# Two levels of the seven-product scheme for the queries of a self-attention stage, and GpSimd in written order

## The chip, the cores and the metric

The kernel runs on one core of one Trainium2 chip. The metric is the device time of one execution in microseconds (us), as the median of several executions. A core has TensorE (PE in the profile, with its weight loads as PEld), VectorE (DVE), ScalarE (ACT), GpSimd (POOL) and SyncE (SP, which here only issues DMAs). Each takes its instructions in order; they wait for one another through semaphores.

## The reference, cut to what matters

One decoder layer in float32: self-attention, cross-attention and a feed-forward part, each followed by a layer norm. The change touches the self-attention, and in it the queries.

```python
# x: 32 x 64 x 512 (2048 tokens); 32 query heads, 8 key/value heads, head size 128
q = (x @ wq.T).reshape(b, l, 32, 128)            # the queries
q, k = apply_rope(q), apply_rope(k)
k_full = concat([k_cache[block_idx], k[0]])      # 512 cached + 64 new keys = 576
v_full = concat([v_cache[block_idx], v[0]])
scores = einsum('bhld,bhtd->bhlt', q, k_full) / sqrt(128)
out = einsum('bhlt,bhtd->bhld', softmax(scores), v_full)
x = layernorm(x + out @ wo.T)
x = layernorm(x + cross_attention(x, ctx_4096))  # not touched
x = layernorm(x + feed_forward(x))               # not touched
```

## The kernel before, in words

**Stages.** Self-attention is the first stage, some 1,800 us of the execution; then come the cross-attention's keys and values, its units, and the feed-forward part. The self-attention's work is cut into 128 *units* n: 8 key groups g, in each 4 token blocks tb of 512 tokens, in each 4 heads h (`REP`). A *block* b is the 4 units of one (g, tb), so there are 32 blocks of four units. Feature-major query tiles `qT` of a block hold 4 heads x 512 tokens.

**A unit.** For each of 4 tiles i of 128 queries: TensorE makes the scores `s` (two matmuls of 288 columns, L834; two PSUM buffers of two banks each), VectorE takes the negated maximum `nmax` (L839), ScalarE the exponential with the sum `den` (L842), VectorE the reciprocal (L851), the scaling of `p` (L857) and a transpose in 32x32 blocks into `T` (L865, `turn`). A tile's transpose is issued after the next tile's maximum. At the unit's end 16 DMAs on SP's queue (`move`, L877) bring `T` to `pT`, and two units later TensorE multiplies it with the values (`po`, L885) in two parts, two or three chunks of 512 columns each. After an odd unit `shared_values` adds the keys that two heads share, and ScalarE copies two heads to `oT` (L908).

**Queries and output projection.** Both are products of 512-wide matrices, in one level of the seven-product scheme (Strassen's in Winograd's form): 7 products of quarters in place of 8. One product is four matmuls of 128x128 weights and 256 moving columns (`Product.mul`, L354). Operand sums are made by GpSimd (`token_sums` for the tokens, `load_left` for the query weights, `output_sums` for the attention's output, `load_right` for wo). The queries of block b + 1 are computed during block b (`q_step`), the projection of an earlier block too (`w_step`). Each of the two has one PSUM bank: tags `q` and `w`. The results are added up by ScalarE copies and VectorE adds, which `flush` issues right after the product (`steps`: at most one product in each of four places of a unit: after the scores of tiles 0, 1, 2 and 3; the values come in before the places 1 and 3).

**Order.** In this stage the order of TensorE, VectorE and ScalarE is the written one (`manual_schedule`); GpSimd's and SP's instructions are put in an order by a planner at build time. In the cross-attention GpSimd's order is the written one as well, and its queries are already made in two levels (`DeepQueries`, L493 to L535): 49 products of 128x128 weights and 128 moving columns, in two sets: 7 steps of four matmuls and 7 steps of three.

Gathers of the next group's cached keys and values are issued on GpSimd's queue in units 4, 5, 6 and 8 of a group; `rotate` (VectorE and GpSimd) turns the keys in unit 9.

Of the kernel before, what the change touches and what calls it, by code (L numbers as in the profile page):

```python
# [9 lines left out]
F32 = mybir.dt.float32  # L10
I32 = mybir.dt.int32
AF = mybir.ActivationFunctionType
ALU = mybir.AluOpType
# [3 lines left out]
P = 128  # L17
DIM = 512
NH, NKV, HD = 32, 8, 128
REP = NH // NKV  # L20
NT = 2048
# [31 lines left out]
def decoder_layer(  # L53
    ctx: ExitStack,
    tc: tile.TileContext,
    x: bass.AP,
    xT_in: bass.AP,
    encT_in: bass.AP,
    cos: bass.AP,
    sin: bass.AP,  # L60
# [63 lines left out]
    def rows(src, tb):  # L124
        return src[tb * TB : (tb + 1) * TB, :].rearrange("(p j) f -> p j f", p=P)
# [150 lines left out]
    def load_right(src, name, eng, queue=nc.sync, first=None, held=None):  # L276

        w = first or load_right_first(src, name, queue)
        for i in range(3, 8):
            w[i] = big.tile([P, 2, HF], F32, tag=f"wo{i}", name=f"{name}_{i}")  # L280
        b12 = w[5]
        for dst, (k, n) in ((w[3], (1, 1)), (b12, (0, 1))):
            load_quarter(dst, src, k, n, queue)
        sums = lambda: right_sums(
            eng, w[1], b12, w[2], w[3], {1: w[5], 2: w[6], 3: w[7], 4: w[4]}
        )
        if held is None:
            sums()
        else:
            held.append(sums)  # L290
        return w
# [390 lines left out]
    with ExitStack() as ph:  # L682
# [2 lines left out]
        psum.append(ph.enter_context(tc.tile_pool(name="sps", bufs=1, space=PSUM)))  # L685
        sc = ph.enter_context(tc.tile_pool(name="sc", bufs=2, space=PSUM))
        sb = ph.enter_context(tc.tile_pool(name="sa", bufs=2))

# [39 lines left out]
        def load_group(g, queue=nc.scalar):  # L730
            ws = []
            for tag, src in (("wk", wkT), ("wv", wvT)):
                w = kv.tile([P, NC, HD], F32, tag=tag, name=f"{tag}{g}", bufs=1)
                queue.dma_start(
                    out=w, in_=src[:, g * HD : (g + 1) * HD].rearrange("(c p) n -> p c n", p=P)
                )
                ws.append(w)
            wkv_cur[g] = ws
# [22 lines left out]
        def gather_values(g, t):  # L761
            gather(g, vs[g], v_rows, t)
# [61 lines left out]
        units = [(g, tb, h) for g in range(NKV) for tb in range(NTB) for h in range(REP)]  # L824
        qTs, Ts, pTs, oTs, pos, ps_ = {}, {}, {}, {}, {}, {}

        def scores(n, i):


            g, tb, h = units[n]  # L830
            u = f"{g}_{tb}_{h}_{i}"
            s = sc.tile([P, 2, 512], F32, tag="sc", name=f"s{u}")
            for a in range(2):
                nc.tensor.matmul(  # L834
                    s[:, a, :HALF], qTs[n // REP][:, units[n][2], i * P : (i + 1) * P],
                    kTs[g][:, a * HALF : (a + 1) * HALF], start=True, stop=True,
                )
            nmax = small.tile([P, 1], F32, tag="nmax", name=f"nmax{u}")
            nc.vector.tensor_reduce(nmax, s[:, :, :HALF], AX.XY, ALU.max, negate=True)  # L839
            p = sb.tile([P, NKEY], F32, tag="p", name=f"p{u}", bufs=4)  # L840
            den = small.tile([P, 1], F32, tag="den", name=f"den{u}")
            nc.scalar.activation(  # L842
                p.rearrange("q (a k) -> q a k", a=2), s[:, :, :HALF], AF.Exp,
                bias=nmax, accum_out=den,
            )
            if i == 0:
                Ts[n] = sb.tile([P, NBK, TPB, SQ], F32, tag="T", name=f"T{g}_{tb}_{h}")
                flush()
            else:
                turn(n, i - 1)  # L850
            nc.vector.reciprocal(den, den)  # L851
            if n < REP or n >= N - REP and i % 2:


                nc.scalar.activation(p, p, AF.Copy, scale=den)  # L855
            else:
                nc.vector.tensor_scalar(p, p, den, None, ALU.mult)  # L857
            ps_[n, i] = p
            if i == TPB - 1:
                turn(n, i)  # L860

        def turn(n, i):


            nc.vector.transpose(  # L865
                Ts[n][:, :, i, :], ps_.pop((n, i)).rearrange("q (b k) -> q b k", k=SQ)
            )
# [56 lines left out]
        def columns(g):  # L924
            return slice(g * REP * HD, (g + 1) * REP * HD)
# [40 lines left out]
        def flush():  # L966
            while reads:
                reads.pop(0)()

        load_group(0, nc.sync)  # L970
        cs2 = kc.tile([P, 1], F32, name="cs2")
        sn2 = kc.tile([P, 1], F32, name="sn2")
# [51 lines left out]
        nc.vector.tensor_tensor(t[4], q[1, 0], t[2], sub)  # L1024
        nc.vector.tensor_tensor(c[0, 1], z, c[0, 1], ALU.add)
        tok[1] = token_operands(xTs[1])
        wo_cur[0] = load_right(woT[columns(0), :], "wo0", nc.gpsimd, first=wo_cur[0])

        def last_products(i):
            if i == 7:  # L1030
# [6 lines left out]
        begin.close()  # L1037

        ph.enter_context(tc.manual_schedule(engines={
            mybir.EngineType.PE, mybir.EngineType.DVE, mybir.EngineType.Activation  # L1040
        }))

        short = {0, 1, 2, *range(N - REP, N - 1)}


        gathers = {4: 0, 5: 1, 6: 2, 8: 3}  # L1050
        for n in range(N):
            b, h = divmod(n, REP)
            g, r = units[n][0], n % PER
            if r == REP and g + 1 < NKV:
                load_group(g + 1)
            if r in gathers and g + 1 < NKV:
                gather_keys(g + 1, gathers[r])
            if 0 < n <= PER:


                b2, j = divmod(n - 1, TPB)
                nc.scalar.dma_start(out=acc[b2][:, j, :], in_=rows(x, b2)[:, j, :])
            if r == 2 * REP and g + 1 < NKV:
                later.append(lambda g=g: new_keys(g + 1))
            if r == 2 * REP + 1 and g + 1 < NKV:
                rotate(g + 1)
                later.append(lambda g=g: cached_keys(g + 1))


            b2, k = b + 2, h - (b == 0)  # L1070
            if b2 < NB and k in (0, 1):
                if k == 0:
                    xTs[b2] = token_room(b2, f"xT{b2}")
                load_pieces(xTs[b2], xT_in, b2 % NTB, 2 * k, 2 * k + 1)
            if n >= N - REP:

                if n == N - REP:
                    encT[0] = big.tile([P, NC, TB], F32, tag="qT", name="encT0", bufs=2)
                    kvw[0], kv_loads, kv_sums = kv_left_parts(0, "wq")
                load_pieces(encT[0], encT_in, 0, h)  # L1080
                for load in kv_loads[3 * h : 3 * h + 3]:
                    load()
                if n == N - 2:
                    kv_sums()
            steps = {0: "qwqw", 1: "qw q", 2: "wqwq", 3: "w qw"}[h]

            def step(place):
                if n < REP:

                    i = {(0, 0): 7, (0, 2): 4}.get((n, place))  # L1090
                    if i:
                        last_products(i)
                        if i == 4:
                            token_sums(xTs[1], "tx1", nc.gpsimd)
                    elif (n, place) in ((0, 1), (0, 3), (1, 0), (1, 1), (1, 2), (2, 0), (2, 2)):
                        q_step(n)
                elif steps[place] == "q":
                    q_step(n)
                elif steps[place] == "w":
                    w_step(b - 2 if h < 2 else b - 1)  # L1100
                flush()

            def spare_bank():

                if n % 2 == 0 and later:
                    later.pop(0)()

            scores(n, 0)
            step(0)
            spare_bank()  # L1110
            scores(n, 1)
            if n - 1 in short:
                move(n - 1, (3,), nc.gpsimd)
            if n >= 2:
                values(n - 2, 0, 2 if n % 2 == 0 else 3)
            step(1)
            scores(n, 2)
            step(2)
            if r in gathers and g + 1 < NKV:
                gather_values(g + 1, gathers[r])  # L1120
            scores(n, 3)
            if n >= 2:
                values(n - 2, 2 if n % 2 == 0 else 3, NKT)
                if n % 2:
                    shared_values(n - 2)
            step(3)
            spare_bank()
            if h == REP - 1:
                if b + 2 < NB:
                    g2, tb2, _ = units[(b + 2) * REP]  # L1130
                    if tb2 == 0:
                        wq_cur[g2] = load_left(wqT[:, columns(g2)], f"wq{g2}", nc.gpsimd)
                    tok[b + 2] = token_sums(xTs.pop(b + 2), f"tx{g2}_{tb2}", nc.gpsimd)
                elif b + 2 > NB:
                    encR[0] = token_sums(encT[0], "te0", nc.gpsimd)
            move(n, (0, 1, 2) if n in short else range(NQD))
# [47 lines left out]
    with ExitStack() as ph:  # L1184
# [6 lines left out]
        bz = cb.tile([P, DIM], F32, name="bz")  # L1191
        pe = cb.tile([P, 1], F32, name="pe")
        wo_cur = {}
        flat = "p a b c -> p (a b c)"
        wl = (
            wqs.rearrange(flat).rearrange("p (j i n) -> p j i n", j=4, i=7),
            cb.tile([P, 3, 7, P], F32, name="wlb"),
# [665 lines left out]
```

## Time and profile before

| | |
|---|---|
| time of 3 runs, median (lowest to highest) | 3007.59 us (3006.82 to 3008.73) |
| the profiled execution's own time | 3004.51 us |
| its span, first to last instruction | 3002.7 us |
| mean granted clock of TensorE | 0.999 of full speed |
| TensorE busy | 2977.4 us, 99% of the span |
| VectorE busy | 2127.5 us, 71% |
| ScalarE busy | 1128.1 us, 38% |
| GpSimd busy | 1218.9 us, 41% |
| DMA, mean over the span | 139 GB/s |

The span is what the trace can be asked about. Busy is the time in which an engine had an instruction under way, without what only issues DMAs or waits on semaphores. In the profile a float32 matmul is two instructions (a product of four matmuls is "x8"). Matmuls overlap in the pipeline, so the cost of one is read from the distance between starts, not from its duration. A line such as `L857 DVE TENSOR_SCALAR p<-p,den` is the operation of line 857 on VectorE which writes tile `p`. "idle before" is time in which the engine waited ahead of the instruction, with what ended the wait.

### The profile page before, as it was taken

The page shows a single profiled execution, that of the slowest core. Times are in us where ns is not written, and L with a number is a line of the kernel's source. Part 1 is how long each engine was busy: PE and PEld are TensorE (multiplying, and loading weights), DVE is VectorE, ACT ScalarE, POOL GpSimd, SP SyncE. Part 2 cuts the span into 40 slices and gives each one's busy share as a digit, 9 for nine tenths or more (in the row PEclk, how much of TensorE's full clock was granted, in tenths as well). Part 3 has the DMA queues.
Part 4 walks back from the last instruction along what each step waited for, and adds up shares of the span by engine and source line. Part 5 has one row for each costly group of instructions (what it writes and reads, how often), then busy time and mean ns, then how long its engine had stood idle before and what let it go on. Part 6 is the DMA issues. An engine that isn't in the chain of part 4 may idle for free.

```text
span 3002.7 us, 46451 instructions
## 1 busy us (share of the span) xinstructions
PE 2977.4 (99%) x16144; PEld 2330.4 (78%) x16144; DVE 2127.5 (71%) x3907; ACT 1128.1 (38%) x2767; POOL 1218.9 (41%) x1024
## 2 busy tenths in 40 slices
PE   8999999999999999999999999999999999999998
PEld 6777777777777777777777768999999999999964
DVE  6787777777787777787787774636656666666686
ACT  4322223223223323323223232334455555555564
POOL 5222322321321321321321223667577577567532
PEclk9999999999999999999999999999999999999999
DMA  6554444444444444444444454666555455445420
GB/s 186 128 131 126 114 115 121 115 115 120 115 115 120 116 114 121 116 114 120 116 115 113 97 124 136 243 247 204 177 179 179 160 183 192 163 160 184 136 81 36
DMA packets 224042, 416.59 MB, mean 139 GB/s; under 512 B 48001, under 2 KB 103425, under 8 KB 215617
## 3 DMA queue, kind: packets, MB, share of 16 engines
q1 hardware_dynamic: 208720, 385.69, 45.0%
q0 software_dynamic: 4304, 19.01, 1.8%
q10 hardware_dynamic: 10784, 8.92, 1.0%
q8 instruction: 130, 2.13, 0.3%
q14 instruction: 104, 0.84, 0.1%
HBM read 206.60 MB, written 33.82 MB: 80 GB/s over the span
## 4 chain that ended last, share of the span: by engine, by line
PE 91%; DVE 3%; POOL 2%; SPq 2%; ACT 1%; DMA 1%; issue 0%; DVEq 0%; ACTq 0%; POOLq 0%
PE po L885 17%; PE s L834 16%; PE sx L1412 2%; PE pox L1495 2%; PE qx_1x L493 2%; PE qx_0x L493 2%; PE qx_2x L493 2%; PE qx_3x L493 2%; PE w_1y L354 1%; PE q_3y L354 1%; PE w_0y L354 1%; PE q_2y L354 1%; PE w_3y L354 1%; PE q_0y L354 1%; PE q_1y L354 1%; SPq L160 1%
## 5 line engine op out<-in xcount | busy, mean ns | idle before, releaser
L842 ACT ACTIVATE p<-s,nmax 128x576 f32<-128x576 f32 x512 | 379.1, 740 | 1210.7 <-DVE nmax L839 1155.4
L834 PE MATMUL s<-kT,qT 128*128 128x288 f32 x2048 | 574.7, 406 | 0.5 <-ACT p L842 0.5
L885 PE MATMUL po<-pT,v 128*128 128x512 f32 (+1 forms) x1280 | 549.0, 602 | 2.4 <-DMA acc<-in_x 1.9
L834 PEld LDWEIGHTS s<-kT,qT 128*128 128x128 f32 x2048 | 387.7, 190 | 100.6 <-issue 17.5
L839 DVE TENSOR_REDUCE nmax<-s 128x1 f32<-128x576 f32 x512 | 384.0, 750 | 58.6 <-PE s L834 57.2
L865 DVE STREAM_TRANSPOSE T<-p 128x576 f32<-128x576 f32 x512 | 394.4, 770 | 12.2 <-ACT p L855 7.4
L885 PEld LDWEIGHTS po<-pT,v 128*128 128x128 f32 (+1 forms) x1280 | 213.4, 189 | 202.0 <-issue 174.8
L857 DVE TENSOR_SCALAR p<-p,den 128x576 f32<-128x576 f32 x488 | 302.0, 619 | 17.1
L325 POOL TENSOR_TENSOR so<-oT,oT 128x512 f32<-128x512 f32 x32 | 40.7, 1272 | 545.3 <-ACT oT L908 545.2
L851 DVE RECIPROCAL den<-den 128x1 f32<-128x1 f32 x512 | 83.9, 164 | 224.8 <-ACT p L842 216.1
L328 POOL TENSOR_TENSOR so<-oT 128x512 f32<-128x512 f32 x32 | 40.7, 1271 | 310.3 <-PE w_1y L354 92.8
L249 POOL TENSOR_TENSOR tx<-xT 128x512 f32<-128x512 f32 x31 | 40.7, 1314 | 199.0 <-PE q_3z L354 63.3
L1444 ACT ACTIVATE exps<-exps,denx 128x64 f32<-128x64 f32 x480 | 121.0, 338 | 0.0
L1515 ACT ACTIVATE oTx<-pox,bv 128x128 f32<-128x128 f32 x248 | 71.1, 490 | 128.3 <-PE pox L1495 128.3
L325 POOL TENSOR_TENSOR sox<-oTx,oTx 128x512 f32<-128x512 f32 x31 | 39.3, 1269 | 149.0 <-DVE oTx L1517 132.4
L535 POOL TENSOR_TENSOR qTx<-d_in 128x512 f32<-128x512 f32 x68 | 85.1, 1274 | 34.7 <-ACT d_in L511 33.3
L842 ACT ACTIVATION_READ_ACCUMULATOR p<-s,nmax 128x1 f32 x512 | 98.7, 193 | 0.0
L535 POOL TENSOR_TENSOR qTx<-d 128x512 f32<-128x512 f32 x60 | 75.1, 1274 | 24.6 <-ACT d L511 23.2
L542 ACT ACTIVATE qTx<-qTx,bq 128x512 f32<-128x512 f32 x128 | 81.9, 713 | 0.0
L1517 DVE TENSOR_SCALAR oTx<-pox,bv 128x128 f32<-128x128 f32 x248 | 70.6, 425 | 14.2 <-PE pox L1495 14.2
L1412 PEld LDWEIGHTS sx<-kv_room,qTx 128*64 128x64 f32 x2048 | 62.3, 138 | 11.1 <-issue 10.1
L908 ACT COPY oT<-po 128x512 f32<-128x512 f32 x128 | 68.2, 587 | 4.1 <-PE po L885 3.8
(590 smaller groups left out, 6217.9 us busy)
## 6 DMA issues: line engine op xcount, KB each, us to landing
pT<-T SPq DMA_DIRECT2D x1016, 80.0 KB
pT<-T SPq DMA_DIRECT2D x1008, 64.0 KB
xT<-tl SPq DMA_DIRECT2D x28, 1792.0 KB
tlb<-tl SPq DMA_DIRECT2D x28, 1344.0 KB
xT<-in_xT SPq DMA_DIRECT2D x123, 256.0 KB
kv_room<-kv SPq DMA_DIRECT2D x32, 512.0 KB
pTx<-Tx SPq DMA_DIRECT2D x256, 64.0 KB
kv<-c SPq DMA_DIRECT2D x28, 512.0 KB
```

Source lines behind the costliest of these rows:

```text
L354: nc.tensor.matmul(self.banks[b][:, m, :], self.left[i][:, k, m * P : (m + 1) * P], self.right[i][:, k, :], start=(first and m + k == 0), ...
L493: nc.tensor.matmul(o[:, j, :], self.left[s][:, j, LEFT[i], :], self.right[s][:, j, RIGHT[i], :], start=(first and j == 0), stop=(j == len( ...
L535: nc.gpsimd.tensor_tensor(self.q[:, :, i, :, v, :], x.rearrange("p (o u) n -> p o u n", o=2), y.rearrange("p (o u) n -> p o u n", o=2), AL ...
L834: nc.tensor.matmul(s[:, a, :HALF], qTs[n // REP][:, units[n][2], i * P : (i + 1) * P], kTs[g][:, a * HALF : (a + 1) * HALF], start=True, s ...
L839: nc.vector.tensor_reduce(nmax, s[:, :, :HALF], AX.XY, ALU.max, negate=True)
L842: nc.scalar.activation(p.rearrange("q (a k) -> q a k", a=2), s[:, :, :HALF], AF.Exp, bias=nmax, accum_out=den,)
L851: nc.vector.reciprocal(den, den)
L857: nc.vector.tensor_scalar(p, p, den, None, ALU.mult)
L865: nc.vector.transpose(Ts[n][:, :, i, :], ps_.pop((n, i)).rearrange("q (b k) -> q b k", k=SQ))
L885: nc.tensor.matmul(pos[n].rearrange("d (a q) -> d a q", a=NQD), vs[units[n][0]][rows, v, :], pTs[n // 2][rows, :, chunk, :], skip_group_ch ...
L1412: nc.tensor.matmul(s[b * SEQ : (b + 1) * SEQ, i * REP + h, :], qTs[n][:, h, pr * HF + c0 : pr * HF + c0 + SEQ], kvs[n][:, pr, 0, c0 : c0 + ...
L1444: nc.scalar.activation(e[:, k, :], e[:, k, :], AF.Copy, scale=den[:, k : k + 1])
```

## The change

**Queries.** From the fifth block on (second key group), the queries of a block are made in two levels, by 14 steps (`SelfQueries.step`): 7 of four 128-column matmuls (set 0), then 7 of three (set 1). All steps use the one bank `q`. Within a set the order is 1, 6, 7, 4, 5, 3, 2. Products 1, 6, 7 and 4 are accumulated on top of one another in the bank, with a ScalarE copy of it after each; 5, 3 and 2 are added to those copies by VectorE. Four (set 0) and three (set 1) GpSimd additions at the end of each set (`post`) make the query tiles, which now lie in another order (`query_block`, `HOMES`).

**Operands.** The 49 left operands of a group (weights, `wdeep`) are made by GpSimd during the third token block of the group before (`first_sums`, `second_sums`). The right operands (tokens) of all four token blocks are made once, in the first group (`token_leaves`, 12 additions and a load and stores for each token block), kept in DRAM, and loaded from there for every block and set into the one room `tq` (`load_tokens`). `acc[2]` and `acc[3]` serve as scratch for that, so half of the loads of `x` into `acc` come later, in units 11 to 14.

**Order.** GpSimd is in written order throughout the stage. `prep` holds GpSimd work in pieces, and one or two pieces are issued at each place (`run_some`). From unit 8 on, the unit is written anew: a projection product after the scores of tiles 0 and 2, and four places for queries, after the scores of tiles 1 and 3 and after the two parts of the values. Place k of head h takes step `idx` = 4h + k, so steps 0 to 13 fill the block but for its last two places. In the places 0 and 2, reciprocal and scaling of tiles 1 and 3 (`scores_last`) come behind the query step on VectorE; matmuls, maximum, exponential and the transpose of the tile before (`scores_first`) come ahead of it. `rotate` runs in two halves. `p` has 3 buffers in place of 4.

The host lays out `x` and wq a second time, in blocks (`xD`, `wqD`).

```diff
+        def scores(n, i):
+            scores_first(n, i)
+            scores_last(n, i)
...
+        HOMES = {(1, 0): 0, (0, 0): 1, (0, 1): 2, (1, 1): 3}
+        SELF_ORDER = (1, 6, 7, 4, 5, 3, 2)
...
+        def token_leaves(tb):
...
+            todo.append(lambda: nc.sync.dma_start(
+                out=raw, in_=xD[tb].rearrange("b p (i n) -> p b i n", i=4)
+            ))
+            todo.append(lambda: None)
+            tt(y2, r22, r12, sub)
+            tt(y1, r12, r11, sub)
+            tt(y3, r22, y1, sub)
+            tt(r12, r21, y3, sub)
+            outer_sums(todo, [tq[:, i, 0:3, :] for i in range(7)], False)
+            a, b = tq_all[tb]
+            todo.append(lambda: nc.gpsimd.dma_start(out=a[:, :, 1:4, :], in_=tq[:, :, 0:3, :]))
+            outer_sums(
+                todo, [raw[:, :, i, :] for i in range(4)] + [more[:, i, :, :] for i in range(3)],
+                False,
+            )
...
+            todo.append(lambda: None)
+            todo.append(lambda: store(nc.sync))
+            todo.append(lambda: None)
+            todo.append(lambda: None)
...
+        class SelfQueries:
...
+            def step(self, s, i):
+                js = 4 - s
+                first = i in (1, 5, 2)
+                if first:
+                    self.bank = bank([P, 4, P], f"{self.name}_{s}{i}", "q")
+                o = self.bank
+                for j in range(js):
+                    nc.tensor.matmul(
+                        o[:, j, :], wdeep[s][:, j, LEFT[i], :], tq[:, RIGHT[i], j, :],
+                        start=(first and j == 0), stop=(j == js - 1), skip_group_check=True,
+                    )
+                k = {1: 0, 6: 1, 7: 3, 4: 2, 5: 3, 3: 1, 2: 0}[i]
+                c, o = self.homes[s][:, :, k, :], o[:, :js, :]
+                if i in (1, 6, 7, 4):
+                    nc.scalar.copy(c, o)
+                else:
+                    reads.append(lambda: nc.vector.tensor_tensor(c, o, c, ALU.add))
...
         ph.enter_context(tc.manual_schedule(engines={
-            mybir.EngineType.PE, mybir.EngineType.DVE, mybir.EngineType.Activation
+            mybir.EngineType.PE, mybir.EngineType.DVE, mybir.EngineType.Activation,
+            mybir.EngineType.Pool,
         }))
...
+            def query(k):
...
+                    if idx < 14:
+                        s, i = divmod(idx, 7)
+                        dqs[nb].step(s, SELF_ORDER[i])
+                        flush()
+                        if i == 3:
+                            load_tokens(nb + s, 1 - s, 0, slice(4, 7))
+                        if i == 6:
+                            dqs[nb].post(s)
+                            load_tokens(nb + s, 1 - s, slice(1, 4))
...
+                run_some(prep, 2 if n < 10 else 1)
+
+            def project(place):
+                if b >= 2 and (h, place) != (1, 1):
+                    w_step(b - 2 if h < 2 else b - 1)
+                    flush()
+                run_some(prep, 2 if n < 10 else 1)
+
+            first_half = 2 if n % 2 == 0 else 3
...
+            else:
+                scores(n, 0)
+                project(0)
+                spare_bank()
+                scores_first(n, 1)
+                query(0)
+                scores_last(n, 1)
...
+                values(n - 2, 0, first_half)
+                query(1)
+                scores(n, 2)
+                project(1)
...
+                scores_first(n, 3)
+                query(2)
+                scores_last(n, 3)
+                values(n - 2, first_half, NKT)
                 if n % 2:
                     shared_values(n - 2)
+                query(3)
```

## The prediction

> **What bounds the kernel now.** I read the page first, then the busy time in stretches of one block (56 us), then the timeline of one unit of a block, and last the timeline of the cross-attention, where two-level queries already run.
>
> ```profile
> PE 2977.4 (99%) x16144; PEld 2330.4 (78%) x16144; DVE 2127.5 (71%) x3907; ACT 1128.1 (38%) x2767; POOL 1218.9 (41%) x1024
> ...
> 1068.00:1124.00 56.00, 56.00 (x218) 40.00 (x217) 43.38 (x78) 16.51 (x38) 15.71 (x12) 1.00 0.48 120
> ```
>
> The columns of the second line are the stretch, its length, busy time of PE, PEld, DVE, ACT and POOL, clock, DMA share and GB/s. TensorE has no gap in a block. Its sum by distances between starts (the timeline from 900 to 960): 16 tiles' scores x 0.97, 7 query and 7 projection products x 1.72, and per pair of units values of 1.72 + 1.72 (two chunks each) and 2.58 + 2.01 (three chunks; one and the shared keys), twice: 15.5 + 24.1 + 16.1 = 55.7 of 56.0 us. So any wait that TensorE gets is paid in full. What it would wait for is read from a unit with h = 2:
>
> ```profile
> 931.89 1.13 PE L834 MATMUL s<-kT,qT 128*128 128x288 f32 x4
> 932.86 1.89 PE L354 MATMUL w_3x<-wo,oT 128*128 128x256 f32 x8
> ...
> 933.37 0.74 DVE L839 TENSOR_REDUCE nmax<-s 128x1 f32<-128x576 f32 x1
> ...
> 934.20 0.74 ACT L842 ACTIVATE p<-s,nmax 128x576 f32<-128x576 f32 x1 [1.94 <-DVE nmax L839]
> 934.58 1.13 PE L834 MATMUL s<-kT,qT 128*128 128x288 f32 x4
> ...
> 935.03 1.27 POOL L329 TENSOR_TENSOR so<-oT,so 128x512 f32<-128x512 f32 x1
> 935.06 0.16 DVE L851 RECIPROCAL den<-den 128x1 f32<-128x1 f32 x1 [0.96 <-ACT p L842]
> 935.26 1.35 DVE L857 TENSOR_SCALAR p<-p,den 128x576 f32<-128x576 f32 x1
> 935.55 1.88 PE L885 MATMUL po<-pT,v 128*128 128x512 f32 x4
> ...
> 936.54 0.68 DVE L553 TENSOR_TENSOR acc<-w_3x,acc 128x512 f32<-128x512 f32 x1
> 937.14 1.21 DVE L561 TENSOR_TENSOR acc<-w_3x,acc 128x1024 f32<-128x1024 f32 x1
> 937.27 1.89 PE L354 MATMUL q_1y<-tx,wq 128*128 128x256 f32 x8
> 938.27 0.74 DVE L839 TENSOR_REDUCE nmax<-s 128x1 f32<-128x576 f32 x1
> ...
> 939.11 0.74 ACT L842 ACTIVATE p<-s,nmax 128x576 f32<-128x576 f32 x1 [4.08 <-DVE nmax L839]
> ```
>
> The second tile's exponential starts 7.2 us after the unit's first scores, since VectorE scales the first tile and adds the projection's product before it takes the second maximum. Today nothing on TensorE waits for that. (The scaling took 1.35 us in place of the usual 0.52: it stood until GpSimd's addition was over.)
>
> ```profile
> 2201.41 0.58 ACT L504 COPY d<-qx_0x 128x512 f32<-128x512 f32 x1 [1.67 <-PE qx_0x L493]
> ...
> 2202.11 0.97 PEld L493 LDWEIGHTS qx_0x<-xT,wq 128*128 128x128 f32 x8
> ...
> 2206.67 1.06 PE L493 MATMUL qx_0z<-xT,wq 128*128 128x128 f32 x8
> 2207.56 1.06 PE L493 MATMUL qx_0x<-xT,wq 128*128 128x128 f32 x8
> 2208.45 0.83 PE L493 MATMUL qx_0x<-tlb,wlb 128*128 128x128 f32 x6
> 2209.12 0.83 PE L493 MATMUL qx_0z<-tlb,wlb 128*128 128x128 f32 x6
> 2209.79 1.89 PE L354 MATMUL wx_1x<-xwo,oTx 128*128 128x256 f32 x8
> ```
>
> A step of four small matmuls takes 0.89 us, of three 0.67. A next step into the same bank starts 0.12 us after the copy of the bank is over (2201.99 to 2202.11); I use 0.13.
>
> **The gain.** A block's queries cost TensorE 7 x 1.72 = 12.04 us now and 7 x 0.89 + 7 x 0.67 = 10.92 after: 1.12 us less, in 28 blocks 31 us. [...]
>
> **What is put in its place: 13 handoffs of one bank.** Each step waits until ScalarE or VectorE has read the step before out of bank `q`. Where a projection, two scores and a copy lie between, that is free. But places 0 and 1, and 2 and 3, of a unit have only values between them. Times from the start of the unit's (or half unit's) first scores, with the trace's distances: maximum 1.17 after scores begin if VectorE is free; exponential 0.84 after that; reciprocal 0.86 later, scaling 0.20, next operation 0.43; an add 0.60, the wide add 1.13; maximum to transpose 0.67, transpose 0.70; ScalarE's next operation 0.87 after the exponential's start; a copy 0.58 (0.48 for three matmuls).
> - Steps 0 to 1 (h = 0): the last transpose of the unit before holds the first maximum to 1.46 (1.48 above). Exponential 2.30, scaling 3.36, projection's add 3.79, second maximum 4.39, its exponential 5.23, copy 6.10 to 6.68, step 1 at 6.81. TensorE is there at 0.97 + 1.72 + 0.97 + 0.89 + 1.72 = 6.27. Wait 0.54.
> - Steps 2 to 3: the same from a free VectorE: copy ends 6.39. Wait 0.25.
> - Steps 6 to 7 (h = 1): this half has no projection, so TensorE is there at 2 x 0.97 + 0.89 + 2.01 = 4.84. VectorE: maximum 1.17, transpose 1.84, reciprocal 2.87, scaling 3.07, maximum 3.50, transpose 4.17, add 4.87 to 5.55, step 7 at 5.68. Wait 0.84.
> - Steps 8 to 9 (h = 2): the projection's first product has two adds: second maximum 3.50 + 0.60 + 1.13 = 5.23, exponential 6.07, copy 6.94 to 7.42, step 9 at 7.55, against 6.05 (a step is now 0.67). Wait 1.5. GpSimd's four additions of `post` (1.27 each, from 5.6 us into the half unit before) and the output sums behind them run just there, and hold up the scaling as above: half an addition on the mean, 0.6. Wait 2.1.
> - Steps 10 to 11: copy ends 6.29, 6.42 against 6.05. Wait 0.37.
> - Steps 4 to 5 and 12 to 13 are VectorE adds that end near 6.15, before three chunks of values are through (7.13 and 6.91). No wait.
>
> Sum 4.1 us a block, net 4.1 - 1.12 = 3.0, in 28 blocks **+84 us**. Below: only 6 to 7 and 8 to 9 without GpSimd's part, 2.3, net 34 us in all. Above: 0.6 more at the three other copies, 5.9, net 134 us.
>
> **GpSimd in written order.** In a steady block it does 7 additions x 1.27 = 8.9 us for 5.3 of token sums now, and in a group 13 for the weights (9 x 1.27 + 4 x 1.06, some 16 us) for 5.2: some 22 of 59 us. `post` of set 1 takes 3 x 1.27 and ends 4.7 us after step 13; the next block's scores come 5.7 us after it. Covered by 1 us; if not, it costs what is over. Gathers and `rotate` wait there for VectorE only, with nothing urgent behind.
>
> The first group is another matter. From unit 1 (30 us) to unit 8 (112 us) GpSimd has three token blocks x (8 x 1.27 + 4 x 1.06), 43 us, and token, wo and output sums, gathers and moves, some 32: 75 of 82 us if it never waits. But the room for raw tokens is single: each next load (1 MB) waits on SP until the stores (1.8 MB, much of it in 512-byte pieces) have landed. The nearest row is the page's `tl<-tlb` store, 1,344 KB in 7.6 us: 10 to 20 us for the stores, 6 for the load, against some 10 us that the empty pieces leave. So GpSimd stands 6 to 16 us three times, with token sums (wanted in units 5 and 8) and `rotate` (its second half on VectorE waits for GpSimd's subtraction in the first) queued behind it, and `pT` moves behind the load on SP. Bounds: 0, if slack takes it, and 75, at 25 each if the moves are late too. I take 10 each: **+30 us**. [...]
>
> **At nothing:** token loads of 3.2 MB a block for 1.0 (40 GB/s more on 120; slices of the cross-attention move 160 to 200), six issues on SP for four; the earliest is wanted 14 us after its issue against 7.6 for the row above. Six ScalarE copies more in a block, 3.3 us of an engine with 16.5 busy in 56. Three buffers of `p`: each is free two maxima before its next use.
>
> **Sum:** 3004.5 + 84 + 30 = 3118.5 for the profiled execution, which lies 3.1 under the median of the runs: **3122 us**. A measurement of this kernel can tell 0.2% (6 us) from no change.
>
> **Rivals.**
> - *The handoffs are covered* (faster): under 1.12 us of waits a block the products decide, and with none it is 3007.6 - 31 = 2976. For it: three pairs miss by 0.25 to 0.54 only. Against: 6 to 7 and 8 to 9 miss by 2.3 with no contention at all. Chance 0.10; no change, the turning point itself, 0.02.
> - *Only these two pairs wait, and the first group has slack*: 3007.6 + 34 = 3042, to 3070 with some of either. 0.13.
> - *The first group decides*: the backlog of GpSimd and SP costs 50 to 75 beside the 84: 3140 to 3170, and near 3215 with the upper bound of the handoffs. For it: 75 of 82 us are full. Against: the work behind is wanted late. 0.17.
> - The forecast, 3080 to 3150: 0.58.
>
> The range leaves out the faster side, no change and the outermost ends: 3045 to 3190. Faster 0.10, same 0.02, slower 0.88.
>
> **What would show it.** Right: blocks of some 59 us; TensorE idle ahead of the query steps, released by ScalarE's copies and VectorE's adds, most at steps 7 and 9; steps of 0.89 and 0.67 us; units 4 to 10 stretched, with GpSimd waiting for the raw load. Wrong: blocks under 56 us; a TensorE without waits ahead of the query steps; or waits on `tq` loads or `pT`, which I cost at nothing.

## The result, and the profile after

The changed kernel takes 3185.36 us (median of four runs, 3182.56 to 3189.72) against 3007.2 us of the kernel before on the same chip: a ratio of 1.0594, 95% interval 1.0576 to 1.0613. It is 178 us slower, where 115 were forecast. The profiled execution has its own time of 3184.07 us and a span of 3182.3, which is 179.6 more than the span before.

The page's line of busy times, of the kernel after:

```profile
PE 3009.8 (95%) x17320; PEld 2353.4 (74%) x17320; DVE 2152.2 (68%) x3949; ACT 1212.4 (38%) x2949; POOL 1475.3 (46%) x1237
```

TensorE falls from 99% to 95% of the span, although its work shrank. To see where, I cut the stage at VectorE's wide addition of a projection's product 1, which comes once a block. This is the answer for those of `w_1x`, first of the kernel before, then of the kernel after (`w_1x` is that addition for block 1 and every fourth block after it, up to block 29; the last two numbers are the first and last start):

```profile
L561 DVE TENSOR_TENSOR acc<-w_1x,acc x8: 1207/1208/1209, 146.8 to 1727.0; 128x1024 f32<-128x1024 f32 x8
```

```profile
L563 DVE TENSOR_TENSOR acc<-w_1x,acc x8: 1208/1208/1209, 190.0 to 1888.8; 128x1024 f32<-128x1024 f32 x8
```

So the 179.6 us lie in three places: 43.2 before the add of block 1 (the first group), 118.6 in the 28 blocks up to block 29 (1698.8 us for 1580.2, that is 60.7 a block for 56.4), and 17.8 behind it. The busy times in these stretches say of what kind they are (columns: stretch, length, busy time of PE, PEld, DVE, ACT and POOL, granted clock, DMA share, GB/s). Before:

```profile
146.80:1727.00 1580.20, 1580.20 (x6170) 1131.96 (x6169) 1236.76 (x2206) 467.57 (x1088) 418.16 (x340) 1.00 0.47 117
20.00:146.80 126.80, 124.76 (x493) 89.39 (x492) 95.70 (x179) 54.44 (x116) 47.43 (x48) 1.00 0.54 142
```

After:

```profile
190.00:1888.80 1698.80, 1598.21 (x7332) 1148.30 (x7331) 1262.64 (x2254) 541.77 (x1255) 606.53 (x495) 0.99 0.56 146
20.00:190.00 170.00, 136.80 (x507) 96.15 (x506) 93.86 (x174) 63.58 (x128) 107.24 (x101) 0.91 0.70 202
```

In the 28 blocks TensorE now stands for 100.6 us, and before for none. It is also busy 18.0 us longer, where its products should have made it 31 us shorter. The clock is no longer 1.00.

The chain of waits gives the idle time to its releasers. TensorE's waits between 190 and 1889 us (what waited, on what; us in total, times, longest):

```profile
PE qd L1122 <- ACT qT L1129: 60.1, 30, 2.6
PE qd L1122 <- DVE tx L1131: 18.2, 27, 0.7
PE qd L1122 <- ACT tx L1129: 8.2, 17, 1.7
PE po L899 <- ACT p L854: 7.5, 4, 2.0
PE po L899 <- DMA pT<-T: 2.8, 2, 1.8
```

86.5 of the 100 us are query steps that wait for the bank's reader, as the prediction said. The largest is step 9. Here is the unit with h = 2 that answers to the one shown of before, from step 7 to the scores after step 9, in the timeline (in brackets the idle time ahead and what ended it):

```profile
975.83 0.94 PE L1122 MATMUL qd<-tq,xT 128*128 128x128 f32 x6 [0.68 <-DVE tx L1131]
...
980.11 1.53 DVE L871 TENSOR_SCALAR p<-p,den 128x576 f32<-128x576 f32 x1
980.27 0.83 PE L1122 MATMUL qd<-tq,xT 128*128 128x128 f32 x6
...
980.93 1.88 PE L899 MATMUL po<-pT,v 128*128 128x512 f32 x4
981.28 1.49 POOL L327 TENSOR_TENSOR so<-oT,oT 128x512 f32<-128x512 f32 x1
...
981.56 0.68 DVE L555 TENSOR_TENSOR acc<-w_2x,acc 128x512 f32<-128x512 f32 x1
...
982.16 1.21 DVE L563 TENSOR_TENSOR acc<-w_2x,acc 128x1024 f32<-128x1024 f32 x1
...
983.29 0.74 DVE L851 TENSOR_REDUCE nmax<-s 128x1 f32<-128x576 f32 x1
...
984.13 0.74 ACT L854 ACTIVATE p<-s,nmax 128x576 f32<-128x576 f32 x1 [4.25 <-DVE nmax L851]
...
984.86 0.47 ACT L1129 COPY qT<-qd 128x384 f32<-128x384 f32 x1
...
985.38 1.65 PE L1122 MATMUL qd<-tq,xT 128*128 128x128 f32 x6 [2.57 <-ACT qT L1129]
...
986.82 2.02 PE L846 MATMUL s<-kT,qT 128*128 128x288 f32 x4
```

It reads from the top: the scaling takes 1.53 us beside GpSimd's additions, then VectorE makes the product's two adds, then the second maximum; ScalarE's exponential waits 4.25 us for that, and the copy that empties bank `q` comes behind the exponential. TensorE had gone on from step 8 to the values at 980.93. The last two lines show something new. Step 9 takes 1.44 us to the next start in place of 0.67, and the scores 1.86 (the next start is 988.68) in place of 0.97: TensorE runs at half pace for about 3 us after the wait. The granted clock in the 6 us after this wait, and in the 6 us after one of 1.83 us ahead of the values at 584.57:

```profile
985.38:991.38 6.00, 6.00 (x23) 5.07 (x23) 2.52 (x6) 1.31 (x3) 1.46 (x1) 0.73 0.58 135
584.57:590.57 6.00, 6.00 (x27) 4.52 (x28) 3.16 (x7) 1.60 (x4) 0.00 (x0) 1.00 0.74 210
```

0.73 over 6 us means 1.6 us lost. The sum of (1 - clock) x 6 us over all 6 us stretches between 190 and 1889 us is **24 us**; before, it is zero.

In the first group GpSimd waits for the raw tokens as forecast, but longer (GpSimd's waits, 20 to 190 us):

```profile
POOL tq L1033 <- DMA acc<-in_xD: 42.6, 3, 19.9
```

and TensorE with it (its waits in the same stretch):

```profile
PE s L846 <- ACT p L854: 12.7, 2, 11.6
PE q_2y L356 <- POOL tx L252: 8.3, 1, 8.3
PE po L899 <- DMA pT<-T: 5.6, 1, 5.6
PE po L899 <- DMA tq<-acc: 4.2, 1, 4.2
```

At 174.5 us the longest of these, 11.6 us on an exponential, goes back to GpSimd too: VectorE stands in the second half of `rotate`, which needs GpSimd's subtraction of the first.

The last block has a wait of its own. GpSimd, in the last units (timeline):

```profile
1952.33 1.26 POOL L244 TENSOR_TENSOR wq<-wq 128x512 f32<-128x512 f32 x1 [7.54 <-DMA wq<-in_xwkv]
...
1957.65 3.94 POOL L891 DMA_DIRECT2D pT<-T  x8
```

The weight sums of the cross-attention (`kv_sums`) stand in written order ahead of the moves of unit 126. They wait for their load, the moves wait with them, and TensorE stands 9.95 us ahead of the values at 1962.52.

### The profile page after: what moved, and what is told of

It reads as the page before. It is cut to its first block, busy times and chain, and to the rows that moved or that the text cites. A ratio compares the mean times of both kernels' runs of the same rounds, so it can differ in the third digit from the quotient of the medians.

```text
span 3182.3 us, 49626 instructions
## 1 busy us (share of the span) xinstructions
PE 3009.8 (95%) x17320; PEld 2353.4 (74%) x17320; DVE 2152.2 (68%) x3949; ACT 1212.4 (38%) x2949; POOL 1475.3 (46%) x1237
## 3 DMA queue, kind: packets, MB, share of 16 engines
q1 hardware_dynamic: 242304, 459.62, 50.3%
## 4 chain that ended last, share of the span: by engine, by line
PE 66%; DVE 13%; DMA 6%; ACT 4%; SPq 4%; POOL 4%; issue 2%; ACTq 0%; DVEq 0%; POOLq 0%
PE s L846 11%; PE po L899 9%; PE qd L1122 8%; DVE nmax L851 4%; ACT p L854 3%; DMA pT<-T 3%; SPq L891 2%; DVE p L871 2%; PE sx L1656 2%; PE pox L1739 2%; PE qx_1x L495 2%; PE qx_0x L495 2%; PE qx_2x L495 2%; SPq L162 2%; PE qx_3x L495 2%
## 5 line engine op out<-in xcount | busy, mean ns | idle before, releaser
L846 PE MATMUL s<-kT,qT 128*128 128x288 f32 x2048 | 593.9, 416 | 12.7 <-ACT p L854 12.7
L899 PEld LDWEIGHTS po<-pT,v 128*128 128x128 f32 (+1 forms) x1280 | 199.8, 191 | 218.9 <-issue 192.9
L871 DVE TENSOR_SCALAR p<-p,den 128x576 f32<-128x576 f32 x474 | 332.3, 701 | 16.6
L1122 PEld LDWEIGHTS qd<-tq,xT 128*128 128x128 f32 x1176 | 157.3, 194 | 171.0 <-ACT qT L1129 106.3
L1122 PEld LDWEIGHTS qd<-tq,wq 128*128 128x128 f32 x1568 | 201.7, 191 | 74.9 <-ACT tx L1129 42.0
L1122 PE MATMUL qd<-tq,xT 128*128 128x128 f32 x1176 | 174.0, 285 | 81.6 <-ACT qT L1129 62.6
L1143 POOL TENSOR_TENSOR qT<-qT,tx 128x512 f32<-128x512 f32 x84 | 110.4, 1343 | 302.5 <-DVE qT L1131 302.5
L1137 POOL TENSOR_TENSOR tx<-tx 128x512 f32<-128x512 f32 x28 | 35.8, 1280 | 452.3 <-ACT oT L922 452.2
L1122 PE MATMUL qd<-tq,wq 128*128 128x128 f32 x1568 | 211.8, 278 | 8.6 <-ACT tx L1129 8.2
L1129 ACT COPY tx<-qd 128x512 f32<-128x512 f32 x112 | 65.1, 581 | 78.1 <-PE qd L1122 78.1
```

The source lines that it names most:

```text
L846: nc.tensor.matmul(s[:, a, :HALF], query_block(n, i), kTs[g][:, a * HALF : (a + 1) * HALF], start=True, stop=True,)
L899: nc.tensor.matmul(pos[n].rearrange("d (a q) -> d a q", a=NQD), vs[units[n][0]][rows, v, :], pTs[n // 2][rows, :, chunk, :], skip_group_ch ...
L1122: nc.tensor.matmul(o[:, j, :], wdeep[s][:, j, LEFT[i], :], tq[:, RIGHT[i], j, :], start=(first and j == 0), stop=(j == js - 1), skip_group ...
L1143: g.tensor_tensor(q[:, v, :, :], q[:, v, :, :], d, add)
```

## The experiments

The theory: the time goes (a) to waits for bank `q` behind ScalarE's order, (b) to the half clock that follows the longer ones, (c) to the one raw room in the first group and (d) to GpSimd's written order in the last block. The rivals: the two-level queries cost something that no order removes (transfers, GpSimd's additions); idle time is all there is, with no clock behind it; GpSimd's written order itself is the cause.

**e1, the copy ahead of the exponential.** In places 0 and 2 the query step and its reader are issued between the tile's maximum and its exponential:

```
 nc.vector.tensor_reduce(nmax, ...)
+if between:
+    between()
 nc.scalar.activation(p, ..., AF.Exp, bias=nmax, ...)
...
-scores_first(n, 1)
-query(0)
+scores_first(n, 1, lambda: query(0))     # and query(2) with tile 3
```

> In the changed kernel, from block 4 on, the query step in places 0 and 2 is issued between the tile's maximum and its exponential, so that the copy out of bank q stands ahead of the exponential in ScalarE's order. Theory (the handoff of the one bank behind the exponential): a copy then ends some 5.0 to 5.3 us after the half unit's first scores, ahead of the values' end at 6.05 to 6.27, so the waits that ScalarE's copies end (62.6 + 8.2 us between 210 and 1935 us of the trace) go, most of VectorE's 18.2 too, and the slow TensorE after the long ones (some 40 us): about 3185 - 125 = 3060, a block near 56 us. Rival (a block is longer for the load on VectorE, DMA or GpSimd, and the wait only shows where it ends): blocks stay above 59.5 us and the time above 3150.

Measured: 3075.0 us (3069.75 to 3079.82), ratio 1.0235 (1.0217 to 1.0252), 15 us more than expected. The 28 blocks take 1594.0 us in place of 1698.8 (busy times, then TensorE's waits, of e1):

```profile
187.90:1781.90 1594.00, 1562.90 (x7331) 1142.58 (x7330) 1250.36 (x2254) 544.89 (x1256) 606.62 (x495) 1.00 0.59 155
```

```profile
PE w_0y L356 <- POOL so L328: 11.5, 7, 3.1
PE po L901 <- ACT p L856: 7.9, 4, 2.3
PE qd L1124 <- DVE qT L1133: 4.7, 6, 0.8
```

No query step waits for ScalarE any more. TensorE is busy 17.3 us less than in the kernel before, and a block without a wait (from 248 to 303 us) takes 54.9 us, where the same kind took 55.9 or 56.0: the step gain of about 1.1 us is there. (a) holds, and it makes 105 of the 178 us, clock included.

**e2, the wide addition behind the scaling.** The second add of projection product 1 is issued after the scaling of tile 1, so that the second maximum comes 1.2 us earlier:

```
+if (h, place) == (2, 0) and len(pj.reads) == 2:
+    wide.append(pj.reads.pop())          # run after scores_last(n, 1)
```

> Only the second, wide add of a projection's first product (h = 2, place 0) is moved behind the scaling of tile 1 on VectorE. It starts 1.13 us of VectorE ahead of the second maximum today. Theory A (a wait near 2.5 us also slows TensorE's clock after it): the wait ahead of step 9 falls from 2.57 to about 1.4 us, 28 x 1.13 = 32 us, and the half-speed matmuls after it go too, 25 to 40 us: 3115 to 3130, mean clock back to 0.99 or more. Theory B (the slow matmuls have another cause): 3153, clock stays near 0.985.

Measured: 3152.63 us (two runs), ratio 1.0487 (1.0466 to 1.0508): theory B's number, with the clock of theory A (mean 0.992). TensorE's waits between 188 and 1862 us:

```profile
PE qd L1122 <- ACT qT L1129: 33.2, 30, 1.4
PE qd L1122 <- DVE tx L1131: 18.8, 28, 0.7
...
PE w_2x L356 <- DVE acc L563: 4.8, 7, 0.7
PE w_3x L356 <- DVE acc L563: 4.8, 7, 0.7
```

The wait ahead of step 9 falls to 1.44 us, and a new one, of 0.7 us, stands ahead of the projection's second product, which needs the bank of the first. So the idle time falls by 9 us only (from 100.6 to 91.5), not by 32, while the 28 blocks take 24.5 us less (189.3 to 1863.6). The rest is the clock: by the same sum it loses 3.4 us in place of 24, and some 6 us of that go to the ends of 24 waits more (107 for 83; the price of an end is worked out below). That is (b), set apart from the idle time: over the 6 us after step 9's wait of 1.44 us (from 1745.16 us, for example) the clock reads 1.00, and after ten of the 14 waits of 2.56 to 2.58 us in the kernel after it reads 0.72 or 0.73.

**e3, GpSimd planned again.** One line, and the planner puts GpSimd in order as it did before:

```
-    mybir.EngineType.Pool,
```

> GpSimd's order in the stage is given back to the planner, all else as in the changed kernel. Theory (in the first group the raw token loads hold up what is written behind them on GpSimd; in the last block the sums of the cross-attention's weights hold up GpSimd's moves): about 13 us come back in the last block, and of the 43 us of the first group as much as the planner puts ahead of the loads, 10 to 40: 3130 to 3165; the steady blocks stay at 60.7. Rival (the order does nothing, the single raw room does): 3172 or above, with TensorE waits of over 8 us still there before 200 us.

Measured: 3180.73 us (two runs), ratio 1.0581 (1.0560 to 1.0602), the same as the change, as the rival had it. Block 1's add comes at 187.2, as in e1, e2 and e4 (187.3 to 189.3), and TensorE's longest wait ahead of it is now 18.0 us, for `pT`; a block takes 61.2 us; the last block falls from 57.0 to 44.5 us, what it was before (43.9). The written order costs something at the end only; giving it up brings nothing of (c) back.

**e4, the last weight sums late.** `kv_sums()` is issued one unit later, behind the moves of unit 126:

```
-    if n == N - 2:
-        kv_sums()
...
+if n == N - 1:
+    kv_sums()
 values(n - 2, 0, first_half)
```

> Only the four GpSimd subtractions and sums for the cross-attention's first weights (kv_sums) are issued one unit later, behind unit 126's moves on GpSimd's queue. Theory: the 9.95 us in which TensorE waits in unit 127 and the slow matmuls after it (2.6 us) go: 3173. Rival (the move itself or its transfer is late): the wait stays, 3185.

Measured: 3170.71 us (two runs, 10 us apart), ratio 1.0548 (1.0526 to 1.0569); the last block takes 44.5 us, the wait of 9.95 us is gone. (d) is settled at 12.5 us, by the time behind block 29 (1281.0 us for 1293.5).

**e5, two raw rooms.** The raw tokens go through `acc[1]` to `acc[3]` in turn, and each load is issued eight pieces into the block before (some loads of `x` into these rooms come later for it):

```
-raw = acc[2]...            ; more = acc[3]...
+raw = acc[(2, 1, 2, 3)[tb]]... ; more = acc[(3, 3, 1, 2)[tb]]...
...
+body.insert(8, leaves[tb + 1][0])        # the next block's raw load
```

> The kernel after, changed only in the first group: the raw token blocks go by turns through idle stretches of the accumulators 1 to 3 in place of always acc[2] and acc[3], and a block's raw load is issued eight pieces into the block before, so that GpSimd's token sums no longer stand behind the stores of the block before. Theory (single raw room sets the first group's loss): TensorE's waits of 4.2, 8.3, 5.6 and 11.6 us between 69 and 175 us go, and with them the half clock that followed each; the add that marks block 1 moves from 190.0 to between 150 and 156 us, steady blocks stay at 60.7 us, and the time falls by 36 to 40 us, to about 3147. Rival (GpSimd and the queues are simply full there: 75 of 82 us): block 1 stays at 180 us or later and the time at 3170 or above.

Measured: 3161.71 us (two runs, 12 us apart), ratio 1.0518 (1.0493 to 1.0542), 24 us less in place of 36 to 40. Block 1's add moves from 190.0 to 169.0, not to 150 to 156. GpSimd's waits for raw tokens and TensorE's waits, 20 to 169 us, of e5:

```profile
POOL tq L1033 <- DMA acc<-in_xD: 13.6, 2, 6.8
```

```profile
PE po L899 <- DMA pT<-T: 10.3, 3, 4.6
PE po L899 <- DMA tq<-acc: 4.2, 1, 4.2
```

The waits on GpSimd and on `rotate` are gone, and those on the moves of `pT` have grown. They are SP's (timeline of its queue, e5):

```profile
65.25 2.60 SPq L1055 DMA_DIRECT2D tq<-acc  x3
68.36 0.36 SPq L1056 DMA_DIRECT2D tq<-acc  x1
68.77 0.52 SPq L1057 DMA_DIRECT2D tq<-acc  x1
69.39 13.09 SPq L891 DMA_DIRECT2D pT<-T  x16
82.52 0.58 SPq L1038 DMA_DIRECT2D acc<-in_xD  x1
```

A unit's 16 moves keep SP for 13.1 us there, of a unit of some 14, so stores and loads push them out. The single room made half of (c); a second bound stood right behind it.

**e6, all of it.** e1, e4 and e5 together, and the next group's wo sums one place later:

```
+wo_cur[g + 1] = load_right(src, name, nc.gpsimd, ..., held=wo_sums)
...
+if (h, place) == (2, 0) and wo_sums:
+    wo_sums.pop()()
```

> The orders of e1 (second step of a pair issued between maximum and exponential) and e4 (last weight sums behind the last but one unit's moves) together, the two raw rooms of e5, and the next group's wo sums issued one place later in their unit, so that GpSimd's output sums do not stand behind the wo load. Theory (the arithmetic saves 1.1 us a block, and everything above that was order): e1's 3075 less 13 (last block) less 36 to 40 (first group) less some 12 to 15 (TensorE's waits for output sums and for rotate's half): 3005 to 3015, blocks at 55.5 to 56.5 us. Below 3001 would be a version that beats the kernel before. Rival (token loads and GpSimd's extra 10 us a block cost something that no order removes): blocks stay at 56.9 us and the time at 3030 or above.

Measured: 3034.49 us (3032.96 to 3036.57), ratio 1.0097 (1.0080 to 1.0113). Busy times of e6:

```profile
20.00:167.90 147.90, 134.68 (x509) 94.84 (x509) 94.31 (x173) 63.59 (x128) 106.60 (x100) 0.94 0.77 222
167.90:1754.10 1586.20, 1559.65 (x7330) 1140.94 (x7329) 1250.14 (x2255) 544.94 (x1256) 608.21 (x495) 1.00 0.60 157
```

The 28 blocks take 1586.2 us, 6.0 more than before: TensorE is busy 20.6 us less and stands for 26.6. The rest of the loss is the first group, 21.1 us up to block 1 and 28 up to block 3. From there to block 29 this kernel and the one before take the same, 1467.3 and 1467.8 us: what the products save goes to 20.4 us of waits, which come once a group (9.9 ahead of the values, mostly for `pT`; 5.5 for wo sums; 4.6 at step 13). The time is the rival's (3030 or above), and the blocks are nearer to its 56.9 than to 55.5 to 56.5. Some 14 us of the miss are those of e5: its 24, not 36 to 40.

**e7, one handoff alone.** The order of e1 at step 8 only:

```
+scores_first(n, 1, (lambda: query(0)) if h == 2 else None)
+if h != 2:
+    query(0)
```

> The kernel after, with the order of e1 at one handoff alone: step 8 is issued between the second maximum and its exponential, so that ScalarE's copy ahead of step 9 no longer stands behind the exponential; steps 0, 2, 6 and 10 stay as they are. It removes the waits ahead of step 9: 60 us of TensorE's 100 between the adds of block 1 and block 29. Theory (a wait of over about 1.85 us also costs the half clock that follows it, 24 us in all by the granted clock, and every wait some 0.26 us of pipeline): 60 + 24 + 7 = 91 us less, about 3094, and a granted clock of 1.00 in nearly all of that stretch. Rival (the idle time is all there is): 3185 less 60, 3125.

Measured: 3130.56 us (3126.61 to 3137.81), ratio 1.0423 (1.0406 to 1.0441), 55 us less: near the rival's number, but not for its reason. Busy times and TensorE's waits of e7:

```profile
188.10:1836.10 1648.00, 1575.99 (x7330) 1136.35 (x7329) 1263.35 (x2253) 542.38 (x1256) 606.16 (x495) 1.00 0.57 150
```

```profile
PE qd L1124 <- ACT qT L1131: 28.9, 26, 1.5
PE qd L1124 <- DVE tx L1133: 18.8, 28, 0.7
```

Both sides of the expectation took it that 60 us of waiting would go. Only 28.6 did (100.6 to 72.0): with step 9 on time, step 11 comes 2.6 us earlier, and now waits 1.1 us for its own copy (489.93 us in the timeline). The 28 blocks fell by 50.3 us all the same (187.8 to 1836.3). 19 of the other 22 are the clock, which loses 5.0 in place of 24 us. So the clock term holds here too; what failed was that a wait taken away leaves nothing behind it.

**e9 and e10, other queues.** e9 is e6 with the first group's stores and raw loads, the first weight loads and the first token loads on GpSimd's queue, and a key gather behind the wo sums. e10 moves all token loads there:

```
-todo.append(lambda: store(nc.sync))
+todo.append(lambda: store(nc.gpsimd))     # raw loads, load_block of group 1 alike
...
-def load_tokens(b, s, *slots, queue=nc.sync):
+def load_tokens(b, s, *slots, queue=nc.gpsimd):    # e10
```

> e6 with the first group's stores and raw loads, the first loads of the weights' blocks and the first tokens' loads issued on GpSimd's queue in place of SP's, and the key gather of the third unit of a group behind the wo sums. Theory (in the first group the moves of pT, 13 us of issue in each unit of 14, stand behind the others on SP): TensorE's waits of 3.6, 2.6, 5.2 and 3.9 us for pT and tq between 69 and 198 us shrink by half or more with the clock that follows them, and the six waits of 0.9 us for wo go: 3034 less 15 to 25, 3010 to 3020. Rival (GpSimd's issue time, 0.5 to 1 us each, takes it back): 3030 or more.

> e9 with all token loads of the two-level queries on GpSimd's queue in place of SP's, six a block. Theory (SP issues 16 moves of 0.8 us in each unit, 52 us of a block's 56, so the six loads fill it up, and pT comes late once a group): the six waits of 0.2 to 2.0 us for pT go, 6 to 12 us below e9, near 3005. Rival (a load that waits on GpSimd for TensorE holds up the output sums behind it): e9's time or more.

Measured: 3037.79 us, ratio 1.0112 (1.0095 to 1.0128), and 3032.17 us, ratio 1.0088 (1.0071 to 1.0105). Both are e6 again. Block 1's add comes at 175 and 172 us, later than in e6. Of the `pT` waits of this part one is now of 8.15 us (e10, at 76.66): units 0 to 2 send a quarter of their moves over GpSimd's queue, and these stand behind its additions, raw loads and stores now. The 28 blocks of e10 take 1584.7 us, TensorE stands for 22.0 of them. So the token loads on SP were not most of what is left in a block, and the first group's loss goes from queue to queue. (The sum in e10's expectation took the first group's 0.8 us a move; in a steady block 16 moves take 10.0 us, 0.63 each.)

No version beats the kernel before. The best, e10, is 0.9% slower.

## Why the prediction was right, and where its sizes were off

The forecast side, its mechanism and its places hold. The sizes hold less well: 3185 lies outside the 3080 to 3150 that was given most of the chance, and 5 us inside the end of the range. That it lies inside is in part luck, for the handoffs came out 28 us under the forecast and three terms at 0 made 60. These are its terms, for the profiled executions, with the measured value and where it is read:

| term | forecast | measured |
|---|---|---|
| 28 blocks, products | -31 | about -1.0 a block, -28 (54.9 against 55.9 in e1 and e6) |
| 28 blocks, handoffs of the bank | +115 (4.1 a block) | +86.5 (the first three rows of the waits) |
| 28 blocks, other waits | 0 | +14 (the rest of 100.6) |
| 28 blocks, beginning and end of a wait | 0 | +22 (83 waits x 0.26, see below) |
| 28 blocks, granted clock | 0 | +24 |
| sum of the 28 blocks | +84 | +118.6 (the terms above give 118.5) |
| first group | +30 | +43.2 |
| behind block 29 | 0 | +17.8, of it 12.5 by `kv_sums` (e4) |

**The handoffs, right.** Step 9 waits 2.56 us or more in half of the blocks and 2.2 on the mean (61.0 us in 28 blocks, 58.4 of them before the add of block 29), where 2.1 was forecast, 0.6 of it for the scaling that stretches beside GpSimd's additions (1.53 us against 0.52). Step 7 waits 0.67 in every block where 0.84 was said; step 1 waits in 16 blocks, mostly 0.28, where 0.54 was said for each. Steps 3 and 11, at 0.25 and 0.37 in the sum, wait four times in all. Step 9's stall gives ScalarE time to catch up: e7 shows that step 11's wait was there behind it, and 1.1 us long, three times the 0.37 of the sum.

**The clock, not counted.** The forecast has no term for the granted clock; the kernel before reads 1.00 in its blocks and in its first 60 us, in spite of a wait of 4.85 us at the start of the trace. That reading shows nothing: the trace's record of the clock begins at 7.75 us, and the product right behind the wait ran slower than the next one of its kind (3.39 us for 1.99; timeline of the kernel before):

```profile
4.85 3.39 PE L354 MATMUL q_0x<-xT,wq 128*128 128x256 f32 x8 [4.85 <-DMA xT<-in_xT]
8.92 1.99 PE L354 MATMUL q_0x<-xT,wq 128*128 128x256 f32 x8 [0.68 <-issue]
```

Here is what five profiles (after, e3 to e5 and e7) show between the adds of block 1 and block 29, by the granted clock of the 6 us that follow a TensorE wait of over 0.9 us: of 78 waits under 1.84 us none is followed by a lower clock; of 42 between 1.84 and 2.3 us 24 are; of 65 between 2.3 and 2.7 us 46; and both longer ones. The lower clock reads 0.72 or 0.73 over the 6 us, about 1.7 us lost each time (0.50 and 3 us after the longest wait, 4.32 us in e3).

In the kernel after, waits of one length that are followed by it and waits that are not differ in where they fall. Its trace's record of the clock has 21 spells of half clock (from 254.74, 316.18 and 497.08 us, for example). They all begin whole multiples of 3.413 us apart, to within 0.005 us, and last 3.41 us or two, three or five times that (the last one, at the end of the execution, is cut short). Cut the time into stretches of 3.413 us at these points, and take for each of the 37 waits of over 0.9 us between 190 and 1889 us the most that it puts into one stretch: 22 put in 1.83 us or less, and none of these is followed by a lower clock; 12 put in 2.0 us or more, and all are; of the three between (1.86, 1.86 and 1.99 us), two are. What makes the clock fall was not shown. The 24 us are those of one execution, with 14 of these spells: e4 and e5, whose steady blocks are the same, lose 30.7 each.

**The ends of a wait, not counted.** I took a wait at the idle time that it shows. But the group before it runs out alone: the values at 980.93 are busy for 1.88 us, where the next start would have come after 1.72. And the first group behind it takes 0.10 us longer (step 7: 0.77 to the next start in place of 0.67). So a wait costs 0.26 us beside what the trace calls idle. The same sum (products -28, idle time, clock, 0.26 a wait) fits the other kernels: +94.7 us for the 28 blocks of e2 (+94.1 measured), +69.6 for e7 (+68.3), +15.1 for e1 (+13.8), +7.9 for e6 (+6.0).

**The first group, right in kind.** GpSimd stood three times for the raw load, but 42.6 us in place of 30, and the clock took another 15 us there, beside TensorE's waits of 33 us, by the same sum over 20 to 190 us, where the prediction has no term for it. It also gave the whole term to the single room. e5 shows that this room makes half (21.0 of 43.2); that SP's queue makes the other is read from its rows.

**The last block, missed.** The prediction went through GpSimd's written order in the steady blocks and in the first group, and not in the last units, where `kv_sums` comes ahead of moves that TensorE waits for. The other 5 us behind block 29 are there in e4 too, with block 30's own handoffs (2.6 and 0.7 us).

**At nothing, in part wrong.** Waits on `pT` were named as a sign of being wrong, and they are there: ahead of the values TensorE waits once a group, seven times in the 28 blocks, 12.1 us in all. (The profile puts 7.5 of it down to exponentials, which the values don't read.) In six of the seven SP stands for about 7 us ahead of the last two of a unit's 16 moves, where before it hardly did (SP's own waits, 147 to 1727 us before and 190 to 1889 us after):

```profile
SPq L877 <- DMA wk<-in_wkT: 5.6, 6, 1.3
SPq L891 <- DMA wk<-in_wkT: 42.7, 6, 7.7
```

Why it stands longer was not tested; the releaser that is named is inferred. GpSimd's `post` and its additions for the weights show in no wait of TensorE there but one of 0.7 us, beside the scaling. Once the handoffs are gone, some of it comes out: in e1 the output sums on GpSimd hold TensorE 11.5 us, once a group.

**The rival that the handoffs are covered** is what e1 builds, and it was priced at 2976. With the handoffs' waits gone, a clean block does save its 1.0 us, but only one block in four comes out clean. The others lose the gain to waits for sums, loads and moves, 26.6 us in e6: it takes 1586.2 us for 28 blocks, where this rival says 1580.2 - 31 = 1549.

What stays open is the remainder of the first group, 21 to 28 us in e6, e9 and e10, and SP's stand ahead of the last moves of a unit once a group. That the first is volume on too few queues is argued from the queues' rows; making the token sums over two groups was not tried.

## What to carry to other kernels

Here, where TensorE had no gap, a wait cost more than the idle time that the trace shows: a quarter of a microsecond at its two ends (0.16 and 0.10), and after 72 of the 109 waits of 1.84 us and more another 1.7 us or so by the clock. So it paid to shorten a wait that could not be removed: with step 9's at 1.44 in place of 2.57 us, e2 lost 3.4 us by the clock in place of 24. Before a product is cut into more and smaller steps in one PSUM bank, follow the bank's reader on its own engine: a copy that is written behind an exponential waits for all that the exponential waits for (4.25 us at 984.13, in the timeline), and to write it ahead was worth 105 us here. And price what stands behind the first bound, and at both ends of a stage: step 11 behind step 9, SP's queue behind the raw room, the last weight sums ahead of the last moves.

## What the runs showed of the hardware that was not expected

The clock's answer to short waits, counted above, was the surprise: a half clock for some 3 us (from 985.38 to 988.68 us in the timeline) after a wait of only 2.57 us, and after none of the 78 under 1.84. Waits of the same length differ: of the 14 between 2.3 and 2.7 us in the kernel after, 10 are followed by it and 4 are not. Three of the four are split by one of the points 3.413 us apart, with less than 1.8 us on either side; the fourth has 1.86 on one side. And a unit's 16 moves, which took SP 10.0 us in a steady block (from 978.34 us, kernel after), took 13.1 in the first group of e5.
